# Moving side work between blocks in a convolution, attention and experts kernel: the last sums' scaling, batch 0's scatter, batch 1's routing steps and batch 0's stores

## The chip, the cores and the metric

The kernel runs on one core of one Trainium2 chip. The metric is device microseconds of one execution, of which the median of three runs is given. A profile is one more execution, taken by the hardware profiler; it has a time of its own.

## The reference, cut to what matters

The input is two images of 256 channels and 56 x 56 positions (3136 tokens each). Layer 0 is an attention without softmax, folded with a normalisation, added to its input and cut at zero. Layer 1 takes the positions as tokens:

```
t = to_tokens(layer0(x))                              # (2, 3136, 256)
t = t + attention(ln(t), W_attn, W_proj)              # 4 heads of 64, causal softmax over 3136 tokens
t = t + experts(ln(t), gate, W1, b1, W2, b2)          # 8 experts 256 -> 512 -> 256, gelu,
                                                      # each token goes to its best two, weighted
out = from_tokens(t)
```

`_L1_attn_ref` computes softmax(q k^T / 8) v by head and projects the result. `_L1_ffn_ref` takes a softmax over the 8 gates, keeps the two largest for each token and adds up the two experts' outputs with those weights.

## The kernel before, in words

All arithmetic is in float32. A token chunk is 128 tokens (25 a batch, the last of 64), a query block 448 tokens (7 a batch).

**Attention (`attend`).** For a batch the loops run over query blocks i, pairs of heads hp (two), and key chunks j. One pass of the innermost loop is a score step: `scores` makes a tile of scores on TensorE (L744), ScalarE takes exponentials into one of five `st` buffers (L752), VectorE masks chunks on the diagonal (L754) and adds the tile to a running sum (L762, L766). Three steps later `values` multiplies with v (L784). At the end of a pair `visit` runs projections of the next block and up to two pieces of output projection (`products`), and `sum_rows` takes the sums of the exponentials over partitions (L808) and sends them to memory in four small transfers and back into another layout (L816, L819). Four score steps later `invert` takes the reciprocals (L828) and sends them out and back spread over partitions (L829, L834); six steps after that `scale` multiplies the attention's output with them (L840); two steps later `hand_on` marks the query block as finished. `due` carries out what has come due on `clock`, which counts score steps.

**Side work.** Everything else that can run beside attention and experts is written as Python generators in `queue`. A generator that yields `True` has done a step that counts, one that yields `False` has nothing to do now and lets the next in the queue have the pull, and `"pe"` stands ahead of TensorE work. `pull(n)` goes through the queue from its front until n steps are counted. In attention `between` pulls one step before each score step. The order in which the Python code issues instructions is the order in which each engine gets them (the engines are under a manual schedule).

**Output projection and routing (`tokens`).** `project_out` projects pairs of chunks once `done()` says that their query block is finished (L682, added to the tokens at L687), and puts a `closer` in the queue, which takes the statistics of one chunk a step (L177, L178). Then `dispatch` does the routing on VectorE: normalisation by Newton's steps (L1061 to L1080), gate softmax (L1083 to L1104, the exponential on ScalarE at L1097), the best two experts (L1117 to L1135), ranks by a matmul (`rank`, L1149 and L1151), and slots (L1153 to L1249). For batch 1, 22 of its points count as a step. Then it scatters the normalised tokens: for each chunk one VectorE operation (L1382, for batch 1 also L1388) and two indirect transfers on GpSimd (L1390) into `x_slots`, with two `xr` buffers for batch 0 and 25 for batch 1. When batch 0 is scattered (`sent`), `tokens` loads the first weights of the eight experts (`w1s`, eight transfers of 512 KB, L1881) and the first rows (L1895).

**Experts (`experts`).** The tokens of an expert are in blocks of 128 rows; 102 blocks run in one loop over n. A pass has `hidden` (16 matmul instructions, L1512, gelu on ScalarE, L1521), `inputs` (turned rows, L1489), `weights` (VectorE copies one expert's w1, taken by a register, L1500), and three blocks behind `outputs` (L1531, bias added by VectorE into one of three `ys`, L1541; stored by SyncE to `y_slots`, L1546, or scattered by GpSimd, L1552). It ends with `between`, which is `meanwhile`: it counts `turn` up by one and pulls from the queue, two steps or, in some phases, more. Blocks up to 41 are of batch 0 alone; rows of block 42 and later need `sent[1]`, which `need(1)` forces when the fetch of their group comes up, six blocks ahead. `side` holds one more generator (`last_blocks`), advanced once a block.

**`closing`** is put at the queue's front when attention ends. It carries the last `later` entries (reciprocal, scaling, handing on) and frees the attention's space for batch 1's scatter.

```python
                    while finished[B - 1][NH - 1] < N:
                        wait = later[0][0] - clock[0]
                        for _ in range(2 * 2 if wait > 4 else 0):
                            yield True
                        clock[0] = max(clock[0], later[0][0])
                        due(clock[0])
```

When attention ends, the reciprocal of the last pair is 3 clock ticks ahead, so it is issued at the first pull; the scaling is 6 ahead and comes after four counted steps; the handing on is 2 ahead and follows at once.

**`finish(0)`** runs from block 57 on: for a pair of chunks it fetches the kept tokens (L1702), gathers four times 128 rows on GpSimd (L1709; `gathered` holds these to one or two a block), adds them up (L1744), and `store` turns them on TensorE (L1757), copies them (L1762) and writes them out (L1763). `finish(1)` does the like for batch 1 and stands ahead of it in the queue. After the last block `settle` empties the queue.

Of the kernel before, what the change touches and what calls it, by code (L numbers as in the profile page):

```python
# [28 lines left out]
def conv_attn_moe_kernel(  # L29
# [52 lines left out]
    P = 128  # L82
# [49 lines left out]
    def pairs(first=0, end=NCH):  # L132

        n = first
        while n < end:
            m = 2 if n + 1 < end and chunk(n + 1) == P else 1
            yield n, m, chunk(n)
            n += m
# [373 lines left out]
    def layer1(nm, general):  # L512

        with ExitStack() as whole:
# [156 lines left out]

            def project_out(b, qT, done):

                for first, m, k in pairs():
                    while done() < (first + m - 1) * P + k:
                        yield False
                    yield "pe"
                    for n in range(first, first + m):
                        o = n * P
                        ps = bank(f"pp_{b}_{n}")  # L680
                        for c in range(NH):
                            nc.tensor.matmul(  # L682
                                ps[:k, : C + E], qT[:, c, o : o + k], wpr[:, c, :],
                                start=(c == 0), stop=(c == NH - 1),
                            )
                        t = ts[b][:k, n, : C + E]
                        nc.vector.tensor_tensor(t, t, ps[:k, : C + E], ALU.add)  # L687
                        if b == 0:
                            nc.sync.dma_start(out=rest_d[:k, n], in_=t[:, :C])
                    if b == 0:  # L690
                        queue.appendleft(closer(b, first, m, k))
                    else:
                        queue.insert(len(queue) - 1, closer(b, first, m, k))
                        yield True
                while unclosed[b]:
                    yield False
# [330 lines left out]
            def dispatch(b):  # L1027
# [349 lines left out]
                for n in range(NCH):  # L1377
                    kk = chunk(n)
                    xr = (scatter_rows[0] if b else bg).tile(
                        [P, width], F32, tag="xr", name=f"xr_{nm}{b}_{n}"  # L1380
                    )
                    nc.vector.tensor_scalar(  # L1382
                        xr[:kk, :C], t[:kk, n, :C],
                        t[:kk, n, MEAN : MEAN + 1], t[:kk, n, RSTD : RSTD + 1],
                        ALU.subtract, ALU.mult,
                    )
                    if b:
                        nc.vector.tensor_copy(xr[:kk, C:], t[:kk, n, C + E - 2 : SLOT + 1])  # L1388
                    for k in range(2):
                        s = nc.gpsimd.indirect_dma_start(  # L1390
                            out=xds[b],
                            out_offset=bass.IndirectOffsetOnAxis(ap=idxs[b][:kk, k, n : n + 1], axis=0),
                            in_=xr[:kk],
                            in_offset=None,
                            bounds_check=xds[b].shape[0] - 1,
                            oob_is_err=False,
                        )
                        group = f"x_slots_{nm}{b}"
                        tc.declare_no_dep(s.ins, group=group, reason="different rows")
                        tc.add_to_no_dep_group(group, s.ins)  # L1400
                        if b or k:
                            yield True
                    if b == 0:
                        yield True
                sent[b] = True

            def experts(w1s, w2s, b2s, ex, es, ps6, between, need, written, settle, decide):
# [282 lines left out]
            def finish(b, oy, bufs):  # L1690
# [57 lines left out]
                        yield True  # L1748

                def store(n, m, k, ys, rows, via=nc.sync):  # L1750
                    w = (m - 1) * P + k
                    ot = oy.tile([P, NH, 2 * P], F32, tag="ot", bufs=2, name=f"ot_{nm}{b}_{n}")
                    yo = bank(f"yo_{b}_{n}", (P, NH, 2 * P))
                    rows = ys[0][:k] if b else rows
                    for o in range(NH):
                        for a in range(m):
                            nc.tensor.transpose(  # L1757
                                yo[:, o, a * P : a * P + k],
                                rows[:, a, o * P : (o + 1) * P],
                                ident[:k, :k],  # L1760
                            )
                    nc.scalar.copy(ot[:, :, :w], yo[:, :, :w])  # L1762
                    via.dma_start(  # L1763
                        out=out[b, :, n * P : n * P + w].rearrange("(c p) n -> p c n", p=P),
                        in_=ot[:, :, :w],
                    )
# [5 lines left out]
                while b == 0 and (parts or ahead):  # L1772
                    if parts:
                        yield from fetch(*parts.popleft())
                    if len(ahead) == bufs or not parts:
                        now = ahead.popleft()
                        yield from add(*now)
                        if added:
                            store(*added)
                            yield True  # L1780
                        added = now
                if b == 0:
                    store(*added)
                    return

# [80 lines left out]

            projected, placed, ranked, sent = ([False] * B for _ in range(4))
            side, worked, scattered = deque(), [0], []
            gathered, turn = [0], [0]
            first, early_rows, scatter_rows, judged = [], [], [], []  # L1870
            last_pool, hots = [], []

            def tokens(b, qT, done):
                yield from project_out(b, qT, done)
                projected[b] = True
                yield from dispatch(b)
                if b == 0:
                    w1s = room(f"w1s_{nm}").rearrange("p (c e h) -> p c e h", c=NH, e=E)
                    first.append(w1s)
                    for e in range(E):  # L1880
                        nc.sync.dma_start(  # L1881
                            out=w1s[:, :, e], in_=w1[e].rearrange("(c p) h -> p c h", p=P)
                        )
                        yield True
                        yield True

                    while not read[B - 1]:
                        yield False
                    for n, m in ((0, 2), (2, 2), (4, 1), (5, 1)):
                        name = f"xb_{nm}_first{n}"  # L1890
                        if m == 2:
                            xb = bg.tile([P, 2, C], F32, tag="xn", name=name)
                        else:
                            xb = bg.tile([P, C], F32, tag="xr", name=name).unsqueeze(1)
                        nc.sync.dma_start(  # L1895
                            out=xb[:, :m],
                            in_=xds[0][n * P : (n + m) * P].rearrange("(n p) w -> p n w", p=P),
                        )
                        early_rows.extend(xb[:, a] for a in range(m))
                        yield True  # L1900
# [132 lines left out]
            def closing():  # L2033

                if not general:

                    while finished[B - 1][NH - 1] < N:
                        wait = later[0][0] - clock[0]
                        for _ in range(2 * 2 if wait > 4 else 0):
                            yield True  # L2040
                        clock[0] = max(clock[0], later[0][0])
                        due(clock[0])
                    while not projected[B - 1]:
                        yield False
                    queue.append(judge())
                end.close()
                scatter_rows.append(pool(spread_rows, "sx", bufs=NCH, side="right"))
                yield True

            queue.appendleft(closing())  # L2050
            with ExitStack() as moe:
# [35 lines left out]
                    queue.appendleft(finish(1, oy, 3))  # L2087

                def meanwhile():
                    gathered[0] = 0  # L2090
                    turn[0] += 1
                    if placed[1] and not sent[1]:
                        pull(2 + turn[0] % 2, every=True)
                    else:
                        pull(
                            4 if worked[0] >= MIXED else 3 if projected[1] and not sent[1] else 2, every=True
                        )
                    if side and next(side[0], None) is None:
                        side.popleft()

                def settle():
                    while queue:
                        gathered[0] = 0
                        pull(every=True)

                def decide():
# [181 lines left out]
```

## Time and profile before

| | |
|---|---|
| median of 3 runs | 1273.84 us (1273.78 to 1274.12) |
| the profiled execution's own time | 1305.54 us |
| its span, first to last instruction | 1303.7 us |
| TensorE matmuls busy | 1259.5 us, 97% |
| VectorE busy | 783.4 us, 60% |
| ScalarE busy | 612.0 us, 47% |
| GpSimd busy | 346.7 us, 27% |
| mean granted TensorE clock | 0.991 |

A line of a timeline has the start in us from the span's start, the length in us, the engine (PE is TensorE, DVE VectorE, ACT ScalarE, POOL GpSimd, SPq SyncE's queue), the line of the kernel, the operation, the tile written and the tiles read, and in brackets the engine's idle time before it with what ended it. A line of the chain of waits has start, length and what was at work; the chain is followed back from the end to what released each step. A row of the table of stretches has for each engine its busy time in the stretch. The ends of matmuls are modelled. Stages by time: layer 0 until about 90 us, batch 0's attention until about 480, batch 1's until 863, experts and the end after that.

### The profile page before, as it was taken

Reading aid. Unit: us, or ns where it says so; the run is one execution under the profiler, and the core shown is the slowest. Engines: PE = TensorE matmul, PEld = TensorE weight load, DVE = VectorE, ACT = ScalarE, POOL = GpSimd, SP = SyncE. Lnnn points to the kernel's source line nnn. Section 1 sums busy time; section 2 is a strip of 40 time slices with the busy share of each in tenths; the row PEclk is TensorE's granted clock in tenths of the full one; section 3 lists DMA queues with packets and bytes.
Section 4 is the critical chain, followed back from the end, with each engine's and each line's share of the span. In section 5 each row is a group of like instructions: output and inputs, shape, how many; then the busy total and the mean of one; then the engine's idle time right before and its main releaser. Section 6 shows DMA issues by size and latency. Waiting matters only on the chain.

```text
span 1303.7 us, 28517 instructions
## 1 busy us (share of the span) xinstructions
PE 1259.5 (97%) x10809; PEld 820.1 (63%) x10809; DVE 783.4 (60%) x1673; ACT 612.0 (47%) x1235; POOL 346.7 (27%) x319
## 2 busy tenths in 40 slices
PE   8999999999999999999999899979999999999997
PEld 7875545544444445454444433449988999899986
DVE  2673566666777744756877677856743443355554
ACT  0255555556565555555555455544332433344432
POOL 1103220000002223311104561000366012666641
PEclk9999999999999999999999999999999999999999
DMA  9994100000000001100001226231344343466743
GB/s 317 352 347 151 32 15 26 24 13 21 13 13 9 25 1 31 27 9 9 10 8 58 81 70 209 79 91 50 98 148 147 90 114 96 147 196 200 210 153 111
DMA packets 111074, 123.87 MB, mean 95 GB/s; under 512 B 19704, under 2 KB 100841, under 8 KB 110931
## 3 DMA queue, kind: packets, MB, share of 16 engines
q1 hardware_dynamic: 100130, 95.18, 24.2%
q0 software_dynamic: 9840, 25.67, 5.9%
q8 instruction: 89, 1.46, 0.5%
q10 hardware_dynamic: 960, 1.11, 0.2%
q14 instruction: 55, 0.44, 0.1%
HBM read 62.06 MB, written 61.05 MB: 94 GB/s over the span
## 4 chain that ended last, share of the span: by engine, by line
PE 92%; DVE 2%; ACT 2%; issue 1%; DMA 1%; another core or an unknown queue 1%; SPq 0%; DVEq 0%; ACTq 0%
PE sc_f L744 20%; PE yp_f L784 20%; PE ht_f L1512 14%; PE yp_f L1531 13%; PE qk_f L614 7%; PE v_f L629 4%; PE pp_f L682 4%; PE cp L410 3%; PE gram L317 2%; PE tp_f L1489 2%; PE sp_f L808 1%; ACT st_f L752 1%; DVE acc_f L766 1%; PE xp_f L600 1%; PE yo_f L1757 1%
## 5 line engine op out<-in xcount | busy, mean ns | idle before, releaser
L766 DVE TENSOR_TENSOR acc_f<-acc_f,st_f 128x896 f32<-128x896 f32 (+5 forms) x372 | 373.7, 1004 | 136.5 <-ACT st_f L752 123.6
L752 ACT ACTIVATE st_f<-sc_f 128x896 f32<-128x896 f32 (+5 forms) x400 | 330.0, 838 | 217.3 <-PE sc_f L744 186.7
L784 PE MATMUL yp_f<-st_f,v_f 64*64 64x448 f32 (+6 forms) x3184 | 338.2, 501 | 3.6 <-DVE st_f L754 1.8
L744 PE MATMUL sc_f<-qT_f,kT_f 64*64 64x448 f32 (+6 forms) x3184 | 336.2, 499 | 5.6 <-ACT st_f L752 5.1
L1521 ACT ACTIVATE g_f<-ht_f,b1b 128x128 f32<-128x128 f32 x408 | 116.6, 372 | 237.2 <-PE ht_f L1512 126.7
L744 PEld LDWEIGHTS sc_f<-qT_f,kT_f 64*64 64x64 f32 x3184 | 118.2, 133 | 160.6 <-issue 138.1
L784 PEld LDWEIGHTS yp_f<-st_f,v_f 64*64 64x64 f32 x3184 | 116.7, 133 | 157.2 <-issue 128.0
L1512 PE MATMUL ht_f<-xT_f,w_f 128*128 128x128 f32 x1632 | 203.7, 278 | 3.1 <-issue 2.2
L1512 PEld LDWEIGHTS ht_f<-xT_f,w_f 128*128 128x128 f32 x1632 | 199.7, 194 | 9.4 <-issue 3.3
L796 POOL TENSOR_TENSOR qT_f<-acc_f 128x448 f32<-128x448 f32 x28 | 32.0, 1142 | 486.3 <-ACT acc_f L795 486.2
L1390 POOL DMA_INDIRECT x_slots<-xr_f,idx x100 | 108.3, 1083 | 135.2 <-DVE xr_f L1388 77.2
L1500 DVE COPY w_f<-w1s_f 128x1024 f32 x102 | 72.6, 712 | 101.2 <-PE ht_f L1512 44.4
L585 POOL TENSOR_SCALAR xn_f<-t 128x256 f32<-128x256 f32 (+1 forms) x50 | 84.9, 1704 | 157.7 <-PE xp_f L600 68.6
L1552 POOL DMA_INDIRECT y_tokens<-ys_f,to_f x57 | 58.5, 1027 | 137.5 <-DVE ys_f L1541 116.6
L614 PE MATMUL qk_f<-px_f,wat 128*128 128x512 f32 (+2 forms) x224 | 88.9, 549 | 4.8 <-ACT st_f L752 4.2
L1541 DVE TENSOR_TENSOR ys_f<-yp_f,kT_f 128x128 f32<-128x128 f32 x102 | 29.5, 289 | 86.0 <-PE yp_f L1531 72.1
L614 PEld LDWEIGHTS qk_f<-px_f,wat 128*128 128x128 f32 x224 | 40.8, 191 | 50.2 <-issue 41.0
L1531 PE MATMUL yp_f<-w2s_f,g_f 128*128 x204 | 61.3, 381 | 1.2 <-issue 1.2
L754 DVE TENSOR_TENSOR st_f<-st_f,keep 128x256 f32<-128x256 f32 (+1 forms) x112 | 45.1, 402 | 28.8 <-ACT st_f L752 26.8
L1531 PE MATMUL yp_f<-kT_f,g_f 128*128 x204 | 61.5, 384 | 0.7 <-issue 0.7
L1531 PE MATMUL yp_f<-px_f,g_f 128*128 x204 | 61.4, 383 | 0.0
L1531 PE MATMUL yp_f<-v_f,g_f 128*128 x204 | 61.1, 381 | 0.0
(285 smaller groups left out, 1224.4 us busy)
## 6 DMA issues: line engine op xcount, KB each, us to landing
x_slots<-fill SPq DMA_DIRECT2D x1, 8190.0 KB
xb_f<-x_slots SPq DMA_DIRECT2D x60, 130.0 KB
x_slots<-fill SPq DMA_DIRECT2D x1, 7296.0 KB
y_slots<-ys_f SPq DMA_DIRECT2D x57, 128.0 KB
kept<-t SPq DMA_DIRECT2D x2, 3200.0 KB
x<-in_x_dram SPq DMA_DIRECT2D x14, 448.0 KB
rb_f<-inverses SPq DMA_DIRECT2D x56, 112.0 KB
y_f<-y_tokens SPq DMA_DIRECT2D x23, 256.0 KB
```

The source lines that it names most:

```text
L585: nc.gpsimd.tensor_scalar(xn[:k, a], ts[b][:k, n + a, :C], ts[b][:k, n + a, MEAN : MEAN + 1], ts[b][:k, n + a, RSTD : RSTD + 1], ALU.subtr ...
L614: nc.tensor.matmul(ps[:, :w], wat[:, c, d0 : d0 + P], px[:, s % 2, c, :w], start=(c == 0), stop=(c == NH - 1),)
L744: nc.tensor.matmul(ps[h : h + HS, a, c0:W], kT[hp][rows, j * P + h : j * P + h + HS], qT[rows, hp, q0 + c0 : q0 + W], start=True, stop=True,)
L752: nc.scalar.activation(st[:k, :, c0:], ps[:k, :, c0:W], AF.Exp, scale=SCALE)
L766: nc.vector.tensor_tensor(acc[:k, :, c0:], acc[:k, :, c0:], st[:k, :, c0:], ALU.add)
L784: nc.tensor.matmul(yp[a * HS : (a + 1) * HS, h // HS, c0:W], v[hp][h : h + HS, j, a, :HS], st[h : h + HS, a, c0:], start=first, stop=bool( ...
L1390: s = nc.gpsimd.indirect_dma_start(out=xds[b], out_offset=bass.IndirectOffsetOnAxis(ap=idxs[b][:kk, k, n : n + 1], axis=0), in_=xr[:kk], i ...
L1500: nc.vector.tensor_copy(w, w1s[:, :, bass.ds(e, 1), :].rearrange("p c e h -> p c (e h)"))
L1512: nc.tensor.matmul(ht[:, k, :], w[:, c, k * P : (k + 1) * P], xT[:, c, :], start=(c == 0), stop=(c == NH - 1),)
L1521: nc.scalar.activation(g[:, k, :], ht[:, k, :], AF.Gelu, bias=b1bs[b][:, k, i : i + 1])
L1531: nc.tensor.matmul(yp[:, :C], g[:, k, :], w2s[k][:, bass.ds(e, 1), :].rearrange("p e d -> p (e d)"), start=(k == 0), stop=(k == KH - 1),)
L1552: s = nc.gpsimd.indirect_dma_start(out=y_tokens, out_offset=bass.IndirectOffsetOnAxis(ap=to[:, n % GB : n % GB + 1], axis=0), in_=ys, in_o ...
```

## The change

Six edits, none of which changes what is computed.

- `project_out` for batch 1 cuts its pairs at chunk 21, where the last query block begins: (20, 1), (21, 2), (23, 1), (24, 1) in place of (20, 2), (22, 2), (24, 1).
- The scatter of batch 0 yields `True` after each of a chunk's two transfers and then `False`; before it yielded once after both, and once more.
- A store of batch 0 waits for the next block if one was issued in this block (`stored`, set back by `meanwhile` and `settle`).
- The loads of w1 take one counted step each, no longer two.
- `closing` waits for three blocks (`turn`) before an entry that is more than 2 ticks ahead, and yields `False` meanwhile. The reciprocal, 3 ahead, so goes into the fourth block's side work, the scaling into the seventh.
- `meanwhile` pulls four steps a block between the end of batch 1's projection and the end of its scatter's first block, no longer three; in its scatter 2, 2, 3 in turn, no longer 2, 3.

```diff
             def project_out(b, qT, done):
 
-                for first, m, k in pairs():
+                ready = (NB - 1) * W // P if b else NCH
+                for first, m, k in (*pairs(0, ready), *pairs(ready)):
                     while done() < (first + m - 1) * P + k:
                         yield False
...
                         tc.add_to_no_dep_group(group, s.ins)
-                        if b or k:
-                            yield True
+                        yield True
                     if b == 0:
-                        yield True
+                        yield False
                 sent[b] = True
...
                 def store(n, m, k, ys, rows, via=nc.sync):
+                    stored[0] += b == 0
...
                         if added:
+                            while stored[0]:
+                                yield False
                             store(*added)
                             yield True
                         added = now
                 if b == 0:
+                    while stored[0]:
+                        yield False
                     store(*added)
                     return
...
-            gathered, turn = [0], [0]
+            gathered, stored, turn = [0], [0], [0]
...
                             out=w1s[:, :, e], in_=w1[e].rearrange("(c p) h -> p c h", p=P)
                         )
-                        yield True
                         yield True
...
                     while finished[B - 1][NH - 1] < N:
-                        wait = later[0][0] - clock[0]
-                        for _ in range(2 * 2 if wait > 4 else 0):
-                            yield True
+                        until = turn[0] + (3 if later[0][0] - clock[0] > 2 else 0)
+                        while turn[0] < until:
+                            yield False
                         clock[0] = max(clock[0], later[0][0])
                         due(clock[0])
...
                 def meanwhile():
-                    gathered[0] = 0
+                    gathered[0] = stored[0] = 0
                     turn[0] += 1
                     if placed[1] and not sent[1]:
-                        pull(2 + turn[0] % 2, every=True)
+                        pull(2 if turn[0] % 3 else 3, every=True)
                     else:
                         pull(
-                            4 if worked[0] >= MIXED else 3 if projected[1] and not sent[1] else 2, every=True
+                            4 if worked[0] >= MIXED or projected[1] and not sent[1] else 2, every=True
                         )
...
                 def settle():
                     while queue:
-                        gathered[0] = 0
+                        gathered[0] = stored[0] = 0
                         pull(every=True)
```

## The prediction

> **What bounds the kernel.** I read the page's busy times first: TensorE is busy 1259.5 us of a span of 1303.7, so a change can only win what TensorE loses: its 44 us of idle time, and the slow matmuls after long idle stretches. The profiled execution took 1305.54 us, 31.7 us more than the median of 1273.84; the sums below are made against the profiled one, and the difference is carried over to the median. Next came the table of stretches, which shows where TensorE is idle.
>
> ```profile
> core 0: us, PE busy (x) PEld busy (x) DVE busy (x) ACT busy (x) POOL busy (x), PEclk, DMA share, GB/s
> 690.00:790.00 100.00, 90.12 (x918) 40.73 (x918) 67.65 (x104) 50.66 (x74) 59.45 (x53) 0.98 0.21 70
> 390.00:490.00 100.00, 98.67 (x950) 45.11 (x950) 63.84 (x92) 56.10 (x80) 21.36 (x15) 1.00 0.05 12
> 870.00:880.00 10.00, 3.43 (x14) 3.23 (x15) 3.49 (x8) 0.42 (x2) 0.00 (x0) 0.74 0.22 64
> ```
>
> From 690 to 790 the scatter of batch 0 (50 indirect DMAs on GpSimd) runs beside batch 1's attention: 9.9 us idle, against 1.3 us in a like stretch of batch 0's attention. From 870 to 880 more than half is idle. The chain of waits names the second:
>
> ```profile
> 865.28 4.95 DMA sums<-sums
> ...
> 870.25 0.21 DVE back_f L828
> ...
> 870.48 1.41 DMA inverses<-back_f
> ...
> 872.40 3.36 DMA rb_f<-inverses
> ...
> 876.57 1.25 PE pp_f L682 x2
> ```
>
> These are the last sums: out to memory, back, reciprocal, out, back, scaled; a projection matmul stands in TensorE's queue behind them. The timeline of TensorE gives the price:
>
> ```profile
> 868.40 1.50 PE L682 MATMUL pp_f<-wpr,qT_f 128*128 128x264 f32 x6
> 876.57 1.25 PE L682 MATMUL pp_f<-wpr,qT_f 128*128 128x264 f32 x2 [6.67 <-DVE qT_f L840]
> 877.61 3.62 PE L1512 MATMUL ht_f<-xT_f,w_f 128*128 128x128 f32 x16
> ...
> 883.31 1.95 PE L1512 MATMUL ht_f<-xT_f,w_f 128*128 128x128 f32 x16
> ```
>
> 6.67 us idle, and then sixteen matmuls take 3.62 us that take 1.95 otherwise.
>
> [...] 2.4 us extra after the 6.67 us, 1.7 us after a wait of 4.16 at 744.77 (four qk and eight pp matmuls, 4.31 us start to start against 2.62). It also shows 1.8 us extra after only 2.09 idle at 1262. [...] The chain's small transfers took 1.41 to 4.95 us each. [...] 0.97 us of a scatter's record plus 0.30 to the next, 1.28, is GpSimd's own rate, which this trace shows from 1002 to 1009.
>
> **Part 1: batch 0's scatter over three steps.** Attention pulls one step per score step, 1.50 us. Before, a chunk puts two scatters (2.56 us of GpSimd) on two steps (3.0 us), 85% of GpSimd before its own additions; after, on three (4.5 us), 57%. No instruction is added. ScalarE's exponentials start 0.7 to 2 us late where scatters follow each other, and TensorE then waits for a score bank. GpSimd is not named as their releaser, and the longest wait (4.21 us) has none. Bounds: nothing gained, if the delay belongs to each scatter or to recording it, up to 9.9 - 1.3 + 1.7 = 10.3. I take 4, under half, because the 31.7 us by which the profiled execution is longer must lie somewhere and such waits are where it could.
>
> What is moved: from the first scatter (in the last steps of query block 4) 98 pulls are left: 6, then 42, then 50. Before: 50 for scatters, 16 for w1, 4 for first rows. After: the third step of each chunk goes to waiting statistics of batch 1; when one such generator runs out, the scatter is advanced in the same pull, so three chunks take 8 pulls, and 25 take 67 (75 at most). Then 8 w1 transfers on 8 pulls and 4 of first rows: done by pull 79 to 87 of 98. w1 (4.2 MB) moves from 791-806 to about 817-827 on SyncE's queue, in front of the sums of the last query block's first half and of the 32 loads of w2 and b2. At the 226 to 244 GB/s of 790-810 all 8 MB land by about 850, before the first expert at 864. The sums queued behind w1 come back later: VectorE's reciprocal can wait 4 us and its scaling 2. VectorE may lag by some three score steps (five st buffers) before ScalarE waits. I take +0.5, bounds 0 and +3. The statistics (0.6 us a chunk) leave 818-851, where VectorE was 98% busy and TensorE lost nothing: no gain.
>
> **Part 2: the last sums.** The reciprocal moves to the fourth block's side work, the scaling to the seventh; TensorE gets expert work instead: -6.67 - 2.4. Chunk 20 alone lies in query block 5, so its projection (1.0 us) goes ahead of the last row sums, where TensorE idles 1.2 us: -1.0. In the seventh block the scaling (0.63) and a projection that needs it come in the same block: TensorE waits for ys, the scaling and the release less the half us of matmuls that need no scaling, +0.7. On SyncE each of the two waits holds y_slots stores for about 2 us, covered by three ys buffers. Sum -9.4; bounds -7 and -10.
>
> **Part 3: batch 1's routing at four steps a block.** It starts three blocks later (block 10, not 7). Its 22 steps are 18 us of VectorE work (rows from 896.3 to 927.2 less copies and additions), 0.81 each. A block is 3.73 us of TensorE, and VectorE has 1.2 us of weight copy and ys in it: three steps make 3.6, four 4.45. The rank matmul waits for the 13th step. Before, rank came one block later; the trace shows how exactly:
>
> ```profile
> 914.04 0.37 DVE L1135 TENSOR_TENSOR both_f<-one_f,one_f 128x200 f32<-128x200 f32 x1
> 914.47 0.07 DVE L1138 MEMSET both_f<- 64x8 f32 x1
> ```
> ```profile
> 914.59 0.60 PE L1149 MATMUL rank_f<-both_f,keep 128*128 128x200 f32 x2
> ```
>
> TensorE was free at 914.55, so nothing was lost. After: block 10 holds step 1; 11 holds 2 to 4 beside one of closing; 12: 5 to 8; 13: 9 to 12; 14: 13 to 16. Step 13 and rank fall into one block. With 0 at the end of block 11's matmuls: VectorE ends steps 2 to 4 at 3.1, copy and ys at 4.2, steps 5 to 8 (0.87, 1.55, 0.55 for the exponential, 1.15) at 8.3, copy and ys 9.4, steps 9 to 12 (4.4) at 13.8, copy and ys 14.9, step 13 at 15.4. TensorE is at rank at 3 x 3.73 = 11.2: a new wait of 4.2, with 1.7 of slow matmuls: +5.9. The same working gives 0.1 for before. Everything behind rank on TensorE, the next block's matmuls, waits. Bounds +2 (VectorE keeps nearly level) and +7.
>
> Batch 1's scatter: 50 steps at 7 per three blocks from block 16 to 37, where before it was 15 to 35. The fetch of block 42's rows comes after side work 37, so nothing is forced; they are used three blocks (11 us) later, against about 5 for the last scatters and 4 for the load. 0, up to +2.
>
> **Part 4: stores.** The page's timeline of the end:
>
> ```profile
> 1261.38 0.98 DVE L1744 SCALAR_TENSOR_TENSOR res_f<-y_f,wt,res_f 64x256 f32<-64x256 f32 x2
> ```
> ```profile
> 1262.46 0.31 PE L1757 MATMUL yo_f<-ident,res_f 64*128 64x64 f32 x2 [2.09 <-issue]
> 1262.70 2.72 PE L1512 MATMUL ht_f<-xT_f,w_f 128*128 128x128 f32 x16
> ```
>
> Three stores fall into one block, and the last waits for its own addition. One a block puts it two to three blocks later, still ahead of the last expert: -2.1 - 1.8 = -3.9; bounds 0 and -4. Elsewhere the gathers (1.5 a block, four a pair) keep stores 2.7 blocks apart, so nothing changes.
>
> **Sum:** -4 + 0.5 - 9.4 + 5.9 - 3.9 = -10.9. Profiled 1305.5 - 10.9 = 1294.6; median 1273.84 - 10.9 = 1262.9, so **1263**.
>
> **Rivals.** (a) More is won: scatter waits go wholly (-10.3 for -4) and VectorE keeps nearly level at rank (+2 for +5.9): 1263 - 10 = 1253. For it: POOL at 57%; against it: the step count above. (b) Less is won: the late starts come with each scatter (0 for -4), and the stores gain only 1.5: 1263 + 4 + 2.4 = 1269. For it: no releaser is GpSimd. With part 3 at +7 and block 42 at +2 as well it is 1272, within 0.2%. (c) **Slower:** w1 lands late. Every first weight copy takes its expert by a register, so it waits for all eight transfers, and TensorE then stands still us for us. If scatters take 75 pulls, w1 stands behind SyncE's own waits (w2's loads were held from 832 to 839 in this trace), starts at 839, and with 6 MB to move at the 146 GB/s of 860-870 ends at 880: 16 us idle + 2.4, less 10.9: 1281. It decides from a landing at about 875 (11 late + 2.4 against 10.9 and the 2.5 us that can be told). Against it: w1 had 240 GB/s beside the same attention.
>
> **Chances.** Forecast 0.50, own range 1258 to 1268; (a) 0.18; (b) at 1269 0.12, at 1272 0.08; (c) 0.12. About 0.2%, 2.5 us, is what a measurement can tell from no change: faster 0.50 + 0.18 + 0.12 = 0.80, same 0.08, slower 0.12. The range 1252 to 1276 leaves out (c) and the far end of (a), under 2 in 10.
>
> **What would show it.** TensorE near 98% in the stretch that holds batch 0's scatter (part 1); no L840 wait at the first experts, chunk 20's pp ahead of sp (part 2); rank_f waiting about 4 us for both_f (part 3; if it waits under 1 us, my step count or VectorE's load is wrong); no yo wait near the end (part 4). The prediction fails if w_f waits for w1, or if a wait of over 3 us stands where I name none.

## The result, and the profile after

| | before | after |
|---|---|---|
| median of 12 runs each | 1274.57 us | 1271.82 us |
| profiled execution's span | 1303.7 us | 1269.3 us |
| TensorE matmuls busy in it | 1259.5 us, 97% | 1247.0 us, 98% |
| mean granted TensorE clock in it | 0.991 | 0.997 |

The ratio is 0.9972, with an interval of 0.9964 to 0.998: about 3.6 us faster (2.75 us between the medians), where 10.9 had been forecast. The two profiles differ by 34 us, ten times as much. That is the first thing to explain: one of the two profiled executions is not like the timed ones. After's is (1271.12 us against a median of 1271.82); before's, 1305.54 us, is not: none of before's twelve timed runs took more than 1277.39.

The table of stretches of the kernel after, with the two stretches that the prediction showed of before; 690 to 790 holds most of batch 0's scatter here too:

```profile
core 0: us, PE busy (x) PEld busy (x) DVE busy (x) ACT busy (x) POOL busy (x), PEclk, DMA share, GB/s
690.00:790.00 100.00, 100.00 (x1078) 45.93 (x1078) 83.97 (x144) 60.26 (x83) 63.73 (x48) 1.00 0.24 77
390.00:490.00 100.00, 98.67 (x950) 45.07 (x950) 63.86 (x92) 56.12 (x80) 21.37 (x15) 1.00 0.04 12
```

TensorE has no idle time left beside the scatter. The chain of waits of the kernel after, where before had the transfers of the last sums:

```profile
866.12 1.74 PE yp_f L1531 x8
...
868.38 0.54 DVE qT_f L841
868.92 0.04 issue
868.96 1.60 PE pp_f L683 x6
```

No transfer is on it any more; it passes VectorE's scaling for half a microsecond. The timeline of TensorE around chunk 20's projection and the scaling (L683 and L809 are L682 and L808 of before):

```profile
845.23 1.16 PE L683 MATMUL pp_f<-wpr,qT_f 128*128 128x264 f32 x4
846.65 0.59 PE L809 MATMUL sp_f<-acc_f,ones 128*32 128x224 f32 x8 [0.27 <-DVE acc_f L767]
...
867.69 0.61 PE L683 MATMUL pp_f<-wpr,qT_f 128*128 128x264 f32 x2
868.96 1.60 PE L683 MATMUL pp_f<-wpr,qT_f 128*128 128x264 f32 x6 [0.67 <-DVE qT_f L841]
```

The projection stands ahead of the row sums, and the new wait in the seventh block is 0.67 us. The rank matmul and the operation that it waits for, on TensorE and on VectorE:

```profile
898.21 0.59 PE L1531 MATMUL yp_f<-w2s_f,g_f 128*128 x2
902.96 1.03 PE L1150 MATMUL rank_f<-both_f,keep 128*128 128x200 f32 x2 [4.16 <-DVE both_f L1139]
903.79 0.87 PE L1152 MATMUL total_f<-both_f,ones 128*128 128x200 f32 x2
904.46 2.73 PE L1512 MATMUL ht_f<-xT_f,w_f 128*128 128x128 f32 x16
```
```profile
902.42 0.37 DVE L1136 TENSOR_TENSOR both_f<-one_f,one_f 128x200 f32<-128x200 f32 x1
902.84 0.07 DVE L1139 MEMSET both_f<- 64x8 f32 x1
```

TensorE is done with the block at 898.8 and waits 4.16 us for the 13th routing step. The end of the kernel after:

```profile
1240.88 0.60 PE L1758 MATMUL yo_f<-ident,y_f 128*128 128x128 f32 x4
1241.41 0.33 PE L1758 MATMUL yo_f<-ident,res_f 64*128 64x64 f32 x2
1241.68 2.05 PE L1512 MATMUL ht_f<-xT_f,w_f 128*128 128x128 f32 x16
```

The last store waits for nothing. So in these two profiles the stalls that the prediction named are where it put them, and gone where it said so; the sizes, and the ground they stand on, were not all right.

### The profile page after: what moved, and what is told of

Same layout as the page of the kernel before. It is cut to its first block, busy times and chain, and to the rows that moved or that the text cites. A ratio compares the mean times of both kernels' runs of the same rounds, so it can differ in the third digit from the quotient of the medians.

```text
span 1269.3 us, 28520 instructions
## 1 busy us (share of the span) xinstructions
PE 1247.0 (98%) x10809; PEld 815.8 (64%) x10809; DVE 783.7 (62%) x1673; ACT 614.4 (48%) x1235; POOL 360.5 (28%) x319
## 4 chain that ended last, share of the span: by engine, by line
PE 95%; DVE 2%; ACT 1%; issue 0%; DMA 0%; DVEq 0%; ACTq 0%
PE yp_f L785 21%; PE sc_f L745 20%; PE ht_f L1512 14%; PE yp_f L1531 13%; PE qk_f L614 7%; PE v_f L629 4%; PE pp_f L683 3%; PE cp L410 3%; PE gram L317 2%; PE tp_f L1489 2%; PE sp_f L809 1%; PE yo_f L1758 1%; PE xp_f L600 1%; DVE acc_f L767 1%; PE tail_f L1623 0%
## 5 line engine op out<-in xcount | busy, mean ns | idle before, releaser
L1512 PE MATMUL ht_f<-xT_f,w_f 128*128 128x128 f32 x1632 | 200.3, 276 | 1.4 <-ACT xT_f L1493 1.4
L1512 PEld LDWEIGHTS ht_f<-xT_f,w_f 128*128 128x128 f32 x1632 | 197.0, 192 | 6.4 <-ACT xT_f L1493 1.8
L1391 POOL DMA_INDIRECT x_slots<-xr_f,idx x100 | 120.7, 1207 | 140.1 <-DVE edge_f L1303 67.1
L1709 POOL DMA_INDIRECT y_f<-y_slots,idx x50 | 57.2, 1144 | 17.2 <-issue 16.9
```

The lines of the kernel that those rows point to most:

```text
L1391: s = nc.gpsimd.indirect_dma_start(out=xds[b], out_offset=bass.IndirectOffsetOnAxis(ap=idxs[b][:kk, k, n : n + 1], axis=0), in_=xr[:kk], i ...
L1512: nc.tensor.matmul(ht[:, k, :], w[:, c, k * P : (k + 1) * P], xT[:, c, :], start=(c == 0), stop=(c == NH - 1),)
```

## The experiments

They came in five series, each on a chip of its own, beside the kernel before. In three of them the kernel before took 1274.75, 1275.07 and 1274.92 us (medians), in the other two 1298.55 and 1298.53. I call these the first and the second kind of chip; whether the cause lies in the chip or in a condition that it keeps for a whole series, the runs do not tell, since no chip was used twice. Ratios are always to the kernel before on the same chip.

### The kernel before again, and three parts alone (first kind)

`before_again` is the kernel before with nothing changed.

> The kernel before, unchanged, profiled a second time. Theory W (the waits with no releaser in the first profile, and most of its 31.7 us over the median, are of that one execution and not of the timed ones): the profiled execution comes within about 5 us of the median, TensorE's 9.9 us of idle time in the stretch of batch 0's scatter shrink to under 2, and the yo wait of 2.09 us at the end is gone; the wait of pp for the scaled qT, 6.7 us and 2.4 us of slow matmuls, stays, since a chain of transfers makes it. Rival S (the waits belong to the kernel's order of work, as my prediction took them in parts 1 and 4): the profile again shows some 10 us idle in that stretch and the yo wait. Ratio 1.000 for both.

Measured: ratio 1.0 (0.9991 to 1.0009), span of the profile 1272.7 us, 31 us shorter than in the first profile. The same stretch in this profile, and TensorE's longest waits in it (in all, times, longest; `issue` means that nothing which the profile shows held the engine up):

```profile
690.00:790.00 100.00, 100.00 (x1074) 45.80 (x1077) 79.06 (x115) 60.28 (x84) 62.02 (x53) 1.00 0.31 101
```
```profile
PE pp_f L682 <- DVE qT_f L840: 6.1, 1, 6.1
PE gram L317 <- DMA xr<-in_x_rows_dram: 3.1, 1, 3.1
PE yo_f L1757 <- issue: 2.1, 1, 2.1
```

The 9.9 us of idle time beside batch 0's scatter are not there, with the same two steps a chunk. The waits at L840 and at the yo matmul are. Theory W was half right: the late starts are of the first profile and not of this one, and the yo wait belongs to the kernel.

`p1_only` is the kernel before with part 1 alone:

```diff
-                        if b or k:
-                            yield True
+                        yield True
                     if b == 0:
-                        yield True
+                        yield False
...
                         )
                         yield True
-                        yield True
```

> The kernel before with part 1 alone (batch 0's scatter over three steps a chunk, w1's loads one step each). Theory W: nothing to win, since the timed executions don't have the waits: ratio 1.000, at most 0.5 us either way. Rival S (the prediction's term): -4 + 0.5, 3.5 us faster, ratio 0.9973; up to 10 us if all of the stretch's idle time goes.

Measured: 1.0003 (0.9994 to 1.0013). Nothing was won.

`p2_only` has the new `closing` and the cut at chunk 21 alone:

```diff
-                for first, m, k in pairs():
+                ready = (NB - 1) * W // P if b else NCH
+                for first, m, k in (*pairs(0, ready), *pairs(ready)):
...
-                        wait = later[0][0] - clock[0]
-                        for _ in range(2 * 2 if wait > 4 else 0):
-                            yield True
+                        until = turn[0] + (3 if later[0][0] - clock[0] > 2 else 0)
+                        while turn[0] < until:
+                            yield False
```

> The kernel before with part 2 alone (reciprocal in the fourth, scaling in the seventh block; chunk 20 projected by itself). Routing then starts at block 10 at the old three steps a block. By the prediction's terms -9.4, less what the rank matmul now waits: worked out with step durations of the trace after, the 13th step falls into the block of rank here too and ends about 3 us after TensorE is there, +1.5 slow matmuls: -9.4 + 4.5 = -5, ratio 0.996. If rank keeps level with VectorE: -9, ratio 0.993. If the wait of 6.7 us was dearer in the first profile than in timed executions (rival C): -1 to -3, ratio 0.998 to 0.999.

Measured: 0.9961 (0.9947 to 0.9975), 5 us (3.2 to 6.8), the number that the terms gave, though not by their sizes, as told below. Its rank matmul does wait, though less than I had worked out (1.9 us for 3), and the matmuls behind it are slow; the timeline of TensorE in `p2_only`:

```profile
903.94 0.61 PE L1150 MATMUL rank_f<-both_f,keep 128*128 128x200 f32 x2 [1.91 <-DVE both_f L1139]
904.39 0.50 PE L1152 MATMUL total_f<-both_f,ones 128*128 128x200 f32 x2
904.72 3.37 PE L1513 MATMUL ht_f<-xT_f,w_f 128*128 128x128 f32 x16
```

`p4_only` has the limit of one store a block alone:

```diff
                         if added:
+                            while stored[0]:
+                                yield False
                             store(*added)
...
```

> The kernel before with part 4 alone (at most one store of batch 0 a block). Theory W: 0, ratio 1.000. Rival S: the yo wait of 2.09 us and 1.8 us of slow matmuls go, -3.9, ratio 0.997.

Measured: 0.9974 (0.9965 to 0.9983). Rival S holds here: the yo wait is gone from its profile and the time with it.

### Variants of the changed kernel (second kind)

> The changed kernel, unchanged, beside its own variants. From the two clean traces the parts give: part 1 0, part 2 -6.9, rank +5.6, stores -3.0 in executions where the matmuls behind the yo wait stay fast and -4.5 where they go slow: -4.3 to -5.8 against the kernel before. The first measurement gave -2.75 (ratio 0.9972). Theory W expects 0.9955 to 0.9975 here; a ratio of 0.999 or more would speak for a cost in the change that its one trace does not show.

Measured: 0.9861 (0.9841 to 0.9881): 1280.82 us against 1298.55. The change is worth 18 us on this chip, where 4.3 to 5.8 had been expected: neither theory knew of a second kind.

`no_p1` is the changed kernel with the diff of part 1 above turned back.

> The changed kernel with part 1 undone (scatter of batch 0 on two steps a chunk, two steps for each w1 load). Theory W (part 1 is worth nothing in timed executions): as the changed kernel, within 0.5 us. Rival S (part 1 wins the prediction's 3.5 us): 3.5 us slower than the changed kernel. Rival L (part 1 costs about 1.5 us, by w1's loads or by the sums queued behind them, and so explains why the changed kernel gains less than its parts): 1.5 us faster than the changed kernel.

Measured: 1294.9 us, ratio 0.9969 (0.9953 to 0.9985). Here part 1, on top of the other parts, is worth 14.1 us, four times rival S's number, and the other parts give 0.9969, as much as the whole change on the first kind. The stretch in `no_p1` and then in the changed kernel, on this chip:

```profile
690.00:790.00 100.00, 90.29 (x910) 39.91 (x910) 67.67 (x104) 50.63 (x73) 61.68 (x53) 0.95 0.22 71
```
```profile
690.00:790.00 100.00, 99.52 (x1066) 45.41 (x1069) 82.73 (x142) 59.57 (x83) 61.07 (x48) 1.00 0.23 77
```

The first line is the first profile of before over again (90.12 us busy there), and that profile's 1305.54 us lies within the 1289 to 1308 us that the kernel before took on this chip. So it looks like an execution of the second kind; on which chip it was taken is not known. What it looks like from near, in `no_p1`: ScalarE, GpSimd and TensorE around 780 (`remote` means that no releaser was found on this core).

```profile
780.32 0.92 ACT L753 ACTIVATE st_f<-sc_f 128x896 f32<-128x896 f32 x1 [2.71 <-PE v_f L629]
783.28 0.92 ACT L753 ACTIVATE st_f<-sc_f 128x896 f32<-128x896 f32 x1 [2.04 <-remote]
```
```profile
777.02 0.98 POOL L1391 DMA_INDIRECT x_slots<-xr_f,idx  x1 [0.30 <-issue]
778.30 1.29 POOL L1391 DMA_INDIRECT x_slots<-xr_f,idx  x1 [0.30 <-issue]
779.89 0.93 POOL L1391 DMA_INDIRECT x_slots<-xr_f,idx  x1 [0.30 <-issue]
781.13 0.92 POOL L1391 DMA_INDIRECT x_slots<-xr_f,idx  x1 [0.31 <-issue]
```
```profile
778.58 2.19 PE L629 MATMUL v_f<-wv,px_f 128*128 128x264 f32 x8
784.58 0.97 PE L809 MATMUL sp_f<-acc_f,ones 128*32 128x224 f32 x8 [3.81 <-ACT v_f L638]
```

ScalarE stands still for 2.71 and 2.04 us ahead of two exponentials, the second time with nothing on this core named as the releaser, while GpSimd goes through indirect transfers with 0.3 us between them; TensorE then waits 3.81 us for the copy of v that is queued behind them on ScalarE.

`no_p3` turns back the two rates in `meanwhile` (three routing steps a block; the scatter 2, 3 in turn).

> The changed kernel with part 3 undone (routing of batch 1 at three steps a block, its scatter 2, 3 in turn). By the trace of part 2 alone, rank then waits 1.9 us with 1.55 us of slow matmuls, not 4.16 and 1.5: 2.2 us faster than the changed kernel, ratio to before about 0.9955. If the prediction's whole term (+5.9) belonged to the rate of four: 5.9 us faster, 0.993.

Measured: 0.984 (0.9816 to 0.9863), 1279.62 us: 1.2 us less than the changed kernel by the medians, 2.7 by the ratios. The two intervals overlap, so the time does not decide between the two expectations. The profile does: rank still waits 1.91 us, and the sixteen matmuls behind it take 3.52 us for 1.95. So most of part 3's term does not belong to the rate of four.

`rank_later` is the changed kernel with a wait for the next block in place of the counted step ahead of rank:

```diff
                 if b:
-                    yield True
+                    until = turn[0] + 1
+                    while turn[0] < until:
+                        yield False
```

> The changed kernel with rank and total put off to the block after the 13th routing step, nothing else. If the 4.16 us wait and the slow matmuls after it are what the rate of four costs: rank finds both done or nearly (TensorE comes to it about 0.4 us before both is ready), -5.2 us against the changed kernel, ratio to before about 0.993. If the wait only moves on (rows a block later are missed at block 42, or another wait takes its place): within 1 us of the changed kernel.

Measured: 0.9824 (0.9804 to 0.9844), 1275.77 us, 5.05 us less than the changed kernel.

### What makes the late starts

Four runs asked it on a chip that turned out to be of the first kind: a third profile of the kernel before (`before_b`), part 1 alone again (`p1_only_b`), and two kernels that take batch 0's indirect transfers out of the kernel before. `no_scatter0` leaves them out; `direct0` puts plain ones in their place: late starts that come with GpSimd's indirect transfers would go in both, late starts that come with the bytes written would go in `no_scatter0` alone. For `direct0_b` and `direct0_c`, the same kernel again, 0.989 stands for the transfers and 1.000 for the bytes. In neither kernel do batch 0's rows come to the places where the experts look for them:

```diff
                     for k in range(2):
-                        s = nc.gpsimd.indirect_dma_start(
+                        if b:
+                            s = nc.gpsimd.indirect_dma_start(
...
+                        else:
+                            nc.sync.dma_start(
+                                out=xds[b][(2 * n + k) * P : (2 * n + k) * P + kk], in_=xr[:kk]
+                            )
```

> The kernel before, a third profile. So far two kinds of chip: of the chips of the calls, one ran it in 1273 to 1278 us, the other in 1289 to 1308, and neither kind has been seen within the other's call. Theory C (a property of the chip: on the second kind engines start late, without a named releaser, while GpSimd issues indirect transfers back to back): the time is either about 1274 with TensorE under 2 us idle from 690 to 800, or about 1298 with some 9 us idle there, and the two go together. Rival R (of the single execution): times or idle between, or both kinds within this call.

Measured: 1.0005 (0.9995 to 1.0015), 1273.0 us of span. Kinds were not mixed within a series: in this one 43 executions of the kernel before took 1271.94 to 1278.02 us.

> The kernel before with part 1 alone, again. Theory C: on the first kind of chip 0 (1.000, as measured there); on the second about 14 us faster, ratio 0.989, which is what undoing part 1 of the changed kernel cost there (1294.9 against 1280.8). Rival E (there it was part 1 together with part 2 that saved the 14 us, with the first weights and the last sums out of each other's way): on the second kind under 5 us.

Measured: 1.0004 (0.9995 to 1.0013): nothing again.

> The kernel before with the 50 indirect transfers of batch 0's scatter left out; VectorE's operations and the steps stay. Batch 0's rows of x_slots so keep the fill. Theory C: on the first kind of chip 0 to -0.5 us; on the second some 14 us faster, as with part 1, since no indirect transfer is left in the stretch. If the late starts there are of other transfers (sums, weights): within 3 us on both.

Measured: 0.9999 (0.9989 to 1.0009). On this kind there is nothing that any spreading could win.

> The kernel before with the 50 indirect transfers of batch 0 replaced by as many plain transfers of the same 128 rows from SyncE's queue, to rows in order (so the places of the rows are not the routing's). Theory C[...]: as with the transfers left out. Rival B (it is the bytes or the writes that disturb): as the kernel before. On the first kind of chip both expect 0 to +1, the latter if the sums' transfers are held behind xr in SyncE's queue.

Measured: 0.9997 (0.9988 to 1.0006).

The same two once more, in a series that was again of the first kind, with `rank_later` beside them:

> Batch 0's indirect transfers left out, again, for a chip that runs the kernel before in 1298 us. Theory C (the late starts come with the indirect transfers): 14 us faster there, 0.989. If they come of something else in the stretch: within 3 us. On the other kind of chip 1.000 once more.

> Plain transfers from SyncE's queue for batch 0's scatter, again, to rows in order, so not at the routing's places. On a chip that runs the kernel before in 1298 us: 0.989 [...], 1.000 if the written bytes do. On the other kind of chip 1.000 once more.

Measured: 0.9996 (0.9987 to 1.0004) and 1.0004 (0.9995 to 1.0012).

> The changed kernel with rank one block later, again. On the chips that run the kernel before in 1274 us: 5.2 us under the changed kernel's 0.9972, so ratio 0.993 (1266 to 1267 us). If the wait has only moved on there: 0.996 or more. On a chip that runs it in 1298: 0.982, as before.

Measured: 0.9926 (0.9912 to 0.9941), 1265.74 us: the fastest of all, 6 us under the changed kernel's median (of another series), and faster than both kernels on both kinds. TensorE at rank:

```profile
903.21 0.60 PE L1152 MATMUL rank_f<-both_f,keep 128*128 128x200 f32 x2 [0.43 <-DVE both_f L1139]
903.66 0.50 PE L1154 MATMUL total_f<-both_f,ones 128*128 128x200 f32 x2
904.00 1.95 PE L1514 MATMUL ht_f<-xT_f,w_f 128*128 128x128 f32 x16
```

0.43 us of wait where I had worked out 0.4, and full speed behind it (1.95 us for the sixteen). From rank's start to the end of these sixteen it is 2.7 us, against 4.2 in the changed kernel.

The last series fell on the second kind:

> Batch 0's indirect transfers left out, for a chip that runs the kernel before in 1298 us: 14 us faster there (0.989) if the late starts come with the indirect transfers, within 3 us if not. On the other kind 1.000.

Measured: 0.9876 (0.9831 to 0.992), 1285.17 us against 1298.53: 13.4 us.

> Plain transfers of the same rows from SyncE's queue, to rows in order. On a chip that runs the kernel before in 1298 us: 0.989 [...], 1.000 if the written bytes do. On the other kind 1.000.

Measured: 0.9897 (0.9851 to 0.9943), 1286.93 us: 11.6 us. The stretch in `no_scatter0_c`, then in `direct0_c`:

```profile
690.00:790.00 100.00, 100.00 (x1074) 45.91 (x1078) 78.54 (x115) 60.25 (x84) 3.42 (x3) 1.00 0.12 35
```
```profile
690.00:790.00 100.00, 100.00 (x1077) 45.77 (x1080) 78.60 (x115) 60.26 (x84) 3.42 (x3) 1.00 0.32 101
```

TensorE is at 100 us in both, where `no_p1`, with the indirect transfers at two steps a chunk and on the other chip of this kind, has 90.29, and in the second the data still moves (101 GB/s against 35). So on the second kind the late starts come with GpSimd's indirect transfers, and not with the amount of data written. `direct0_c` changes two things at once, though: SyncE issues the transfers, and the rows go in order and not to the routing's places. Whether it is GpSimd's issuing or the scattered places, these runs do not show. By which road ScalarE is delayed, and why one kind of chip shows it and the other does not, no run here shows. Part 1 alone was not run on the second kind; that the kernel before has 13.4 us to win there without part 2 speaks against a share of part 2 in the 14.1.

Part 1 does not make the two kinds equal: `no_scatter0_c` still takes 10.5 us more than `no_scatter0` and the changed kernel 9 us more than on the first kind. In `no_scatter0` rank starts at 898.44 and the first matmul of `tail_f` at 1256.12, in `no_scatter0_c` at 898.11 and 1267.42. So the rest, 11.6 us in these two profiles, is lost among the experts, where GpSimd issues batch 1's scatter, the scattered outputs and the gathers. No run takes those out, and whether they are the cause is open.

## Why the prediction was wrong

**Part 1 is the step that failed:** "I take 4, under half, because the 31.7 us by which the profiled execution is longer must lie somewhere and such waits are where it could." On the kind of chip that the median is of, the term is 0, by four measurements within 0.05% of no change (part 1 alone twice, the transfers left out twice). On the other it is -14.1. Under half is true of neither: I saw that the profile and the median did not belong together, and took a value between two conditions in place of deciding which one the forecast was for. What could have been told is a budget. TensorE's idle time of 44.2 us in the first profile is 26.3 in `before_again` (1272.7 less 1246.4 busy); the other 13 us of the 31 are longer busy time of the same 10809 matmuls. If the timed executions are 31.7 us shorter, a large part of the 44.2 and of the slow matmuls beside it must go. Which part, the page could not tell: the longest late start has no releaser on this core, but neither has the yo wait (`issue`), and that one came back in every profile of a kernel with its stores as before. A second profile told it.

The sign that the prediction set for part 1, TensorE near 98% beside the scatter, came true (100 us of 100) and means nothing, since `before_again` has the same 100. Rival (b), with 0.20 of the chance, has 0 for -4, and 1272 at its far end, which is the time measured. That is luck: its reason, late starts that come with each scatter, holds on neither kind (there are none on the first, and spreading won 14.1 us on the second), the stores gained more than its 1.5, part 3 did not reach 7, and block 42 cost nothing that the spans show. "Carried over to the median" was the same fault in general: sizes were taken from the disturbed execution.

**w1's loads** (+0.5) cost nothing that can be told: `p1_only` holds them too. Measured from the end of attention at 848 they were issued some 52 to 47 us ahead (795.6 to 801), where I had put them 47 to 37 ahead; w_f never waits for them, and rival (c) fell. That a first weight copy would wait for all eight transfers was my reading of the program; no run tested it.

**Part 2 is the second step, mis-sized: mechanism right, size too large.** -9.4 was forecast. The eighth group of outputs matmuls starts at 896.07 in `before_again` and at 888.94 in `p2_only`; less the 0.23 us by which attention ended earlier there, that is -6.9. The wait for L840 was 6.05 us, not 6.67; the sixteen matmuls behind it took 2.95 us, 1.0 too much and not 1.67; a wait that I did not name appeared, 0.61 us of L1512 for xT, where a projection used to stand between two blocks. The prediction's figures were those of a dear execution: in nine profiles of the first kind with this wait it is 5.67 to 6.64 us, and the sixteen take 2.86 to 3.62. The new wait of 0.7 in the seventh block came out at 0.67, and chunk 20's projection fills the idle time ahead of sp as said. The 5 us of `p2_only` agree with the terms by luck: its trace gives -6.9 and, at rank, +1.9 and +1.4, so -3.6.

**Part 3: right in sum, its cause not.** +5.9 was forecast as 4.2 of wait and 1.7 of slow matmuls. The wait is 4.16, and the durations of rank, total and the sixteen behind them add up to 4.63 us where `rank_later_b` has 3.05: 1.58 more. Taking the wait away won 5.05 us on the second kind. But the term had two causes that I had put on one: part 2 alone, at three steps, makes a rank wait of 1.9 with 1.4 of slow matmuls behind it (3.37 for 1.95), because routing begins at another step of the block.

**Part 4: right in place, too large in most executions.** -3.9 was forecast as 2.1 of wait and 1.8 of slow matmuls. `p4_only` gained 3.3 us by the ratio (2.2 to 4.5). The wait is 2.08 or 2.09 us in every profile that has it, but what follows it varies, see below; in `before_again` nothing behind it is slow. There the trace gives -2.2: the sixteen matmuls ahead of which both kernels have done the same stores start at 1244.90, in `p4_only` at 1243.11, with 0.42 for the later start of rank there. The -3.0 in the expectation of `after_again` is too large: I had compared at a point where `p4_only` still had two of those stores to do.

**The sum** from profiles of the first kind: 0 - 6.9 + 5.7 - 2.2 = -3.4, and -3.4 between the spans of `before_again` and after; 3.6 measured by the ratio. Of the 7.3 us between forecast and ratio, part 1 with w1's loads is 3.5, part 2's size 2.5 and part 4's 1.7; part 3 takes back 0.2, and the last 0.2 are within the measurement.

## What to carry to other kernels

If the profiled execution is longer than the median by more than the gain you look for, profile again before a term is sized on its waits. That a wait has no named releaser is not enough to strike it out: here the late starts were gone in the next profile (9.9 us of idle time, then none), and the yo wait came back every time (2.08 or 2.09 us). A change that clears a wait also moves all that follows in the queue: look for the next place where two engines must meet in the same block, since a wait of 4 us there gave back more than half of what had been won, and one block of distance won it back (5.05 us).

## What the runs showed of the hardware that was not expected

The late starts beside batch 0's indirect transfers are told above: without the transfers the kernel before was 13.4 us faster on the second kind of chip (`no_scatter0_c`), and no faster on the first (ratios 0.9999 and 0.9996).

The kernel before runs at two levels on the first kind, below 1275 and above 1276 us, with few runs between (8 of 137). Two profiles with the same yo wait, one from each level, differ behind it: first `before_again` (1274.37 us), then `p1_only` (1276.88 us).

```profile
1233.21 0.30 PE L1757 MATMUL yo_f<-ident,res_f 64*128 64x64 f32 x2 [2.08 <-issue]
1233.45 2.05 PE L1512 MATMUL ht_f<-xT_f,w_f 128*128 128x128 f32 x16
```
```profile
1234.46 0.36 PE L1756 MATMUL yo_f<-ident,res_f 64*128 64x64 f32 x2 [2.08 <-issue]
1234.74 3.59 PE L1511 MATMUL ht_f<-xT_f,w_f 128*128 128x128 f32 x16
```

The same idle time of 2.08 us, and the matmuls behind it take 2.05 us once and 3.59 the other time. From 1233 to 1240 the granted clock is 1.00 in the first and 0.76 in the second. The other profiles of the first kind with the stores as before, `p2_only` apart, fit: five executions of 1273.04 to 1274.79 us have 2.05 us there, and `direct0` at 1278.06 us has 3.11. What decides between the two, no run shows. Where the yo wait is gone, the upper level is too: `p4_only` ran from 1271.85 to 1273.31, the changed kernel from 1271.11 to 1273.18. So the price of a wait of 2.08 us varies here (2.05 to 3.59 us for the same sixteen matmuls), and with it goes some of the spread. It is not the whole of the two levels: of the 2.5 us between the two profiles about half lies ahead of the wait, and `p2_only`, which keeps the wait, ran from 1269.72 to 1271.24 in all five of its runs.
